# Joining neighbouring short rows into one stored tile, in a pairwise outer-product kernel with batch normalisation

## The chip, the cores and the metric

The kernel runs on one core of a Trainium2 chip. The metric is the device time of one execution in microseconds (us), the median over several runs. Beside it there is one profiled execution, which gives the busy time of the engines (TensorE, VectorE, ScalarE, GpSimd and SyncE, written PE, DVE, ACT, POOL and SP in the profile) and of the transfers.

## The reference

Inputs are `xi` and `xj`, each (1024, 39, 16) in float32: 1024 samples, 39 fields, 16 values. For every pair of fields (r, c) with c < r, 741 pairs in all, the outer product of `xj[:, r]` and `xi[:, c]` is formed, a 16 x 16 block. Each pair is normalised over the samples and the block, scaled by `gamma`, shifted by `beta` and multiplied by one 16 x 16 matrix `W`.

```
rows, cols = tril_indices(39, k=-1)                    # 741 pairs
cross  = xj[:, rows, :, None] * xi[:, cols, None, :]    # (1024, 741, 16, 16)
mean   = mean(cross, axis=(0, 2, 3))
var    = mean((cross - mean)**2, axis=(0, 2, 3))
normed = (cross - mean) * rsqrt(var + 1e-5) * gamma + beta
out    = normed[:, None] * W                            # (1024, 1, 741, 16, 16)
```

The output is 1024 x 741 x 256 x 4 bytes = 777 MB. The inputs are 5 MB.

## The kernel before

**Tiling.** The 1024 samples lie on 128 partitions with 8 samples each. The pairs are taken by row: row r has r pairs, (r, 0) to (r, r-1), and they stand next to each other in the output. A tile is one row for T = 2 of the 8 samples of every partition, so that it holds 2r blocks of 1 KB per partition. A row takes four tiles, for the samples `t0` = 0, 2, 4 and 6.

**The buffer.** All tiles live in one tensor, `y_sb`, of 2 x 76 blocks per partition. Its two halves (`slot`) are used in turn. In each half lie a long row r and the short row 38-r behind it, 38 pairs per sample together, so that a half is always full. The list `tiles` says for each tile its row, its first sample and its place. The order is first the middle row 19, then 20 with 18, then 38 alone, then 37 with 1, 36 with 2, down to 21 with 17. Within a pair of rows it goes long, short, long, short, with `t0` growing. A place is used again by the tile four steps later.

**The work of a tile.** `scale_xi` (GpSimd) multiplies `xi` by the pair's scale into a small tile `xs`, of which there are two. `products` forms the blocks: for each sample and each i of 16 one instruction multiplies `xs` by a scalar of `xj`. ScalarE and GpSimd divide the 16 between them (`split`). Rows 5 to 7 are formed whole on GpSimd, rows 1 to 4 on VectorE. `finish` adds the shift and multiplies by `W`. VectorE does most pairs, each with one `scalar_tensor_tensor` for both samples. A share (`POOL_SHARE`, 0.13 of the row, rounded) is done on GpSimd. `store` then issues the DMAs on SyncE. A tile of a row up to 19 leaves in one DMA for both samples, a longer one in one DMA for each sample. Rows over 30 leave in two pieces, with the last sample stored whole where the row is 36 or less.

**The order.** Nothing is reordered: each engine runs its instructions as they were written. One loop over the tiles writes them, and each step of it forms the products of the tile ahead while the present one is finished:

```
for n in range(1, len(tiles)):
    if n + 2 < len(tiles):
        scale_xi(n + 2)
    finish(n)
    ...          # apply(group), where its tile has come
    if n + 1 < len(tiles):
        products(n + 1)
```

Waits come from overlaps of the regions read and written: the products of a tile wait for the stores that read its place last, and a store waits for the engines that finished its tile.

**Statistics.** Ahead of the loop the means and variances of all pairs come from sums over samples and small matrix products. `spread` copies the coefficients to all partitions by groups of rows (`ROW_GROUPS`), and `apply`, three or four small VectorE instructions, turns a group's coefficients into scale and shift. In the kernel before, each group names the tile at which it is applied.

Line numbers in the profile are those of the kernel before: L148 and L150 are the products on ScalarE and GpSimd, L170 is `scale_xi`, L231 is the store, L294 and L297 are GpSimd's share of `finish`, and L308 is VectorE's.

Of the kernel before, what the change touches and what calls it, by code (L numbers as in the profile page):

```python
# [7 lines left out]
F32 = mybir.dt.float32  # L8
AF = mybir.ActivationFunctionType
ALU = mybir.AluOpType  # L10
# [4 lines left out]
T = 2  # L15
# [12 lines left out]
SHORT, OWN = 4, 1  # L28
# [3 lines left out]


ROW_GROUPS = (
    (19, 20, 0, None), (20, 21, 1, None), (18, 19, 1, 2), (38, 39, 1, 8), (34, 38, 1, 9), (1, 5, 1, 10), (29, 34, 2, 36),
    (5, 10, 2, 37), (25, 29, 3, 76), (10, 14, 3, 77), (21, 25, 4, 108), (14, 18, 4, 109),
)
SHORT_GROUP = 5

# [2 lines left out]
def tile_pair_outer_batchnorm(  # L42
# [24 lines left out]

    half = T * (F - 1)
    mid = (F - 1) // 2
    tiles = [(mid, t0, t0 // T * half // 2) for t0 in range(0, NT, T)]  # L70
    slot = 0
    for r in (mid + 1, *range(F - 1, mid + 1, -1)):
        for t0 in range(0, NT, T):
            tiles.append((r, t0, slot * half))
            if r < F - 1:
                tiles.append((F - 1 - r, t0, slot * half + T * r))
            slot ^= 1

    RAW = 1

# [1 line left out]
    scaled_short = ctx.enter_context(tc.tile_pool(name="scaled_short", bufs=1))  # L82
    scaled = ctx.enter_context(tc.tile_pool(name="scaled", bufs=2))
    psp = ctx.enter_context(tc.tile_pool(name="ps", bufs=1, space=bass.MemoryType.PSUM))
    xi_sb = cpool.tile([P, NT, F, E], F32, name="xi_sb")
    xj_sb = cpool.tile([P, NT, F, E], F32, name="xj_sb")
    w_sb = cpool.tile([P, 1, EE], F32, name="w_sb")
    st_sb = cpool.tile([P, 2, NP], F32, name="st_sb")
    s_sb = st_sb[:, 0:1].unsqueeze(3)
    t_sb = st_sb[:, 1]  # L90
    y_sb = cpool.tile([P, 2 * half, EE], F32, name="y_sb")
    w_dve = psp.tile([P, 1, EE], F32, name="w_dve")

    xi_v = xi.rearrange("(p t) f e -> p t f e", t=NT)
    xj_v = xj.rearrange("(p t) f e -> p t f e", t=NT)
    out_v = out.rearrange("(p t) o n i j -> p t (o n i j)", t=NT)


# [37 lines left out]
    stt = nc.vector.scalar_tensor_tensor  # L136

    def view(n):
        r, _, u = tiles[n]
        return y_sb[:, u : u + T * r, :].rearrange("p (t n) e -> p t n e", t=T)  # L140

    def product(n, engine, t, i, src):

        r, t0, _ = tiles[n]
        y = view(n).rearrange("p t n (i j) -> p t n i j", j=E)[:, t, :, i, :]
        scale = xj_sb[:, t0 + t, r, i : i + 1]
        if engine is nc.scalar:
            nc.scalar.activation(y, src, AF.Copy, scale=scale)  # L148
        else:
            engine.tensor_scalar(y, src, scale, 1.0, ALU.mult, ALU.mult)  # L150

    def raw_products(n, engine, steps):
        r, t0, _ = tiles[n]
        for step in steps:
            t, i = divmod(step, E)
            yield lambda t=t, i=i: product(n, engine, t, i, xi_sb[:, t0 + t, 0:r, :])

    def emit(work, count):
        for _, step in zip(range(count), work):
# [2 lines left out]
    xs_of = {}  # L162

    def scale_xi(n):
        r, t0, _ = tiles[n]
        if r <= SHORT:
            return
        n0 = first[r]
        xs = scaled.tile([P, T, r, E], F32, tag="xs", name=f"xs_{r}_{t0}")
        nc.gpsimd.tensor_tensor(  # L170
            xs,
            xi_sb[:, t0 : t0 + T, 0:r, :],
            s_sb[:, :, n0 : n0 + r, :].to_broadcast([P, T, r, E]),
            ALU.mult,
        )
        xs_of[n] = xs

    def products(n):

        r, t0, _ = tiles[n]  # L180
        if r <= SHORT:
            xs = scaled_short.tile([P, T, r, E], F32, tag="xs_short", name=f"xs_{r}_{t0}")
            nc.vector.tensor_tensor(  # L183
                xs,
                xi_sb[:, t0 : t0 + T, 0:r, :],
                s_short[:, first[r] : first[r] + r]
                .unsqueeze(1)
                .unsqueeze(3)
                .to_broadcast([P, T, r, E]),
                ALU.mult,  # L190
            )
            for t in range(T):
                nc.vector.tensor_tensor(  # L193
                    view(n)[:, t].rearrange("p n (i j) -> p n i j", j=E),
                    xs[:, t].unsqueeze(2).to_broadcast([P, r, E, E]),
                    xj_short[:, t0 + t, r - 1 : r, :].unsqueeze(3).to_broadcast([P, r, E, E]),
                    ALU.mult,
                )
            return
        xs = xs_of.pop(n)  # L200
        if r <= OUTER:
            for t in range(T):
                nc.gpsimd.tensor_tensor(  # L203
                    view(n)[:, t].rearrange("p n (i j) -> p n i j", j=E),
                    xs[:, t].unsqueeze(2).to_broadcast([P, r, E, E]),
                    xj_sb[:, t0 + t, r : r + 1, :].unsqueeze(3).to_broadcast([P, r, E, E]),
                    ALU.mult,
                )
            return
        if n < 3:  # L210
            split = E - POOL_I_FIRST[n]
        elif r > LONG:
            split = E - POOL_I_LONG
        else:
            split = E - (POOL_I_BESIDE if SHORT < F - 1 - r <= OUTER else POOL_I)
        for t in range(T):
            for i in range(E):
                product(n, nc.scalar if i < split else nc.gpsimd, t, i, xs[:, t])

    def store(n, c0, c1, t_from=0, t_to=T):  # L220
        r, t0, _ = tiles[n]
        n0 = first[r]

        whole = n >= len(FIRST_PIECES) and r <= WHOLE
        step = 1 if r > mid and (whole or c1 == r) else t_to - t_from
        for t in range(t_from, t_to, step):
            if whole and step == 1 and t == t_to - 1:
                if c1 < r:
                    continue
                c0 = 0  # L230
            nc.sync.dma_start(  # L231
                out_v[:, t0 + t : t0 + t + step, (n0 + c0) * EE : (n0 + c1) * EE],
                view(n)[:, t : t + step, c0:c1, :].rearrange("p t n e -> p t (n e)"),
            )

    def affine(n, pairs, engines=(nc.scalar, nc.gpsimd)):

        r = tiles[n][0]
        y = view(n)
        for c in pairs:  # L240
            s_c = st_sb[:, 0, first[r] + c : first[r] + c + 1]
            t_c = t_sb[:, first[r] + c : first[r] + c + 1]
            engine = engines[c % len(engines)]
            if engine is nc.scalar:
                nc.scalar.activation(y[:, :, c, :], y[:, :, c, :], AF.Identity, bias=t_c, scale=s_c)  # L245
            else:
                engine.tensor_scalar(y[:, :, c, :], y[:, :, c, :], s_c, t_c, ALU.mult, ALU.add)  # L247
# [14 lines left out]
    def bounds(n):  # L262
        if n < len(FIRST_PIECES):
            return FIRST_PIECES[n]
        r = tiles[n][0]
        if r <= ONE:
            return 0, r

        return 0, r // 2 + max(0, (WHOLE + 1 - r) * 3 // 2), r

    def finish(n):


        r = tiles[n][0]
        n0 = first[r]
        y = view(n)
        long = r > LONG
        p1 = r // 2 if long else r
        if long:
            share = POOL_PAIRS_LONG  # L280
        elif RAW < n < 10:
            share = POOL_PAIRS_FIRST
        else:
            share = int(r * POOL_SHARE + 0.5) if r > SHORT else 0
        p0 = p1 - share
        step = POOL_PAIRS_LONG // 2 if long else r
        for c0 in range(p0, p1, step):
# [30 lines left out]
    with tc.manual_schedule():  # L318
# [2 lines left out]
        def load(engine, to, source, t):  # L321
            engine.dma_start(to[:, t], source[:, t])

        nc.sync.dma_start(xi_sb[:, 0, 0 : F // 2], xi_v[:, 0, 0 : F // 2])
        nc.scalar.dma_start(xi_sb[:, 0, F // 2 : F], xi_v[:, 0, F // 2 : F])
        load(nc.sync, xj_sb, xj_v, 0)
        load(nc.scalar, xi_sb, xi_v, 1)
        load(nc.sync, xj_sb, xj_v, 1)
# [19 lines left out]

        sources = (xj_sb[:, :, 1:F], xi_sb[:, :, 0:G])
        scales = (0.25, 0.25 / NB**0.5)

        def field(x, k):
# [123 lines left out]
        used = [0] * len(ps_st)  # L478

        def spread(group):  # L480
            r0, r1, bank, _ = ROW_GROUPS[group]
            n0, n1 = first[r0], first[r1 - 1] + r1 - 1
            at = used[bank]
            used[bank] = at + 2 * (n1 - n0)
            ps = ps_st[bank][:, at : used[bank]].rearrange("p (x n) -> p x n", x=2)
            for r in range(r0, r1):
                nc.tensor.matmul(  # L487
                    ps[:, :, first[r] - n0 : first[r] - n0 + r],
                    pick[:, r - 1, :],
                    stq[:, :, 0:r],  # L490
                    start=True,
                    stop=True,
                )
            spread_of.append((ps, n0, n1))
# [23 lines left out]
        products(1)  # L518
        scale_xi(2)

        for n in range(1, len(tiles)):
            if n + 2 < len(tiles):
                scale_xi(n + 2)
            finish(n)
            for group, (_, _, _, tile_of) in enumerate(ROW_GROUPS):
                if n == tile_of:
                    apply(group)
            if n + 1 < len(tiles):
                products(n + 1)
            if n == 12:  # L530
                nc.scalar.copy(xj_short, xj_sb[:, :, 1 : SHORT + 1, :])


# [26 lines left out]
```

## Time and profile before

| | |
|---|---|
| median of 3 runs | 1863.88 us (1863.8 to 1863.93) |
| the profiled execution's own time | 1864.56 us |
| its span, first to last instruction | 1862.7 us |
| VectorE busy | 1714.3 us, 92% |
| ScalarE busy | 1576.3 us, 85% |
| GpSimd busy | 1542.9 us, 83% |
| TensorE busy | 34.3 us, 2% |
| written to HBM | 776.99 MB, 420 GB/s over the span |
| packets | 55286 in all, 54928 on SyncE's queue |
| chain that ended last | DMA 53%, ACT 22%, DVE 18%, issue 3% |

Busy time is the time in which an engine has an instruction in it; the mean duration that the profile gives for one instruction is longer than its share of the busy time, since neighbours overlap. A packet is what one DMA engine moves as one piece. The time to landing of a DMA runs from its issue to the signal that it has ended, so that it holds the wait behind earlier transfers. The chain is followed back from the last instruction, at each step to what released it.

### The profile page before, as it was taken

Reading aid. Unit: us, or ns where it says so; the run is one execution under the profiler, and the core shown is the slowest. Engines: PE = TensorE matmul, PEld = TensorE weight load, DVE = VectorE, ACT = ScalarE, POOL = GpSimd, SP = SyncE. Lnnn points to the kernel's source line nnn. Section 1 sums busy time; section 2 is a strip of 40 time slices with the busy share of each in tenths; the row PEclk is TensorE's granted clock in tenths of the full one; section 3 lists DMA queues with packets and bytes.
Section 4 is the critical chain, followed back from the end, with each engine's and each line's share of the span. In section 5 each row is a group of like instructions: output and inputs, shape, how many; then the busy total and the mean of one; then the engine's idle time right before and its main releaser. Section 6 shows DMA issues by size and latency. Waiting matters only on the chain.

```text
span 1862.7 us, 9385 instructions
## 1 busy us (share of the span) xinstructions
PE 34.3 (2%) x212; PEld 33.7 (2%) x212; DVE 1714.3 (92%) x2638; ACT 1576.3 (85%) x3130; POOL 1542.9 (83%) x1655
## 2 busy tenths in 40 slices
PE   7000000000000000000000000000000000000000
PEld 7000000000000000000000000000000000000000
DVE  8999889899999999999999999999999999999994
ACT  8999888888888776666898989999999998989891
POOL 9999777787777789999988888888888888888882
PEclk7555555555555555555555555555555555555555
DMA  7999999999999999999999999999999999999998
GB/s 289 396 421 421 430 427 427 429 424 427 424 428 423 424 424 426 427 425 425 420 428 429 428 430 427 426 427 427 427 431 427 426 428 431 428 425 428 428 428 359
DMA packets 55286, 783.60 MB, mean 421 GB/s; under 512 B 4784, under 2 KB 6448, under 8 KB 18096
## 3 DMA queue, kind: packets, MB, share of 16 engines
q1 hardware_dynamic: 54928, 782.53, 99.2%
q14 instruction: 69, 0.57, 0.1%
q10 hardware_dynamic: 288, 0.48, 0.1%
q8 instruction: 1, 0.02, 0.0%
HBM read 6.00 MB, written 776.99 MB: 420 GB/s over the span
## 4 chain that ended last, share of the span: by engine, by line
DMA 53%; ACT 22%; DVE 18%; issue 3%; POOL 1%; PE 0%; SPq 0%; ACTq 0%; DVEq 0%; POOLq 0%
DMA out_dram<-y_sb 53%; ACT y_sb L148 22%; DVE y_sb L308 17%; POOL y_sb L150 1%; DVE y_sb L364 0%; POOL xs L170 0%; POOL y_sb L247 0%; PE ps L401 0%; SPq L231 0%; DVE y_sb L254 0%; ACTq L148 0%; PE ps L379 0%; DVE y_sb L385 0%; DVE y_sb L371 0%; DVE xs L183 0%
## 5 line engine op out<-in xcount | busy, mean ns | idle before, releaser
L308 DVE SCALAR_TENSOR_TENSOR y_sb<-y_sb,st_sb,w_dve 128x512 f32<-128x512 f32 (+1 forms) x2511 | 1653.1, 740 | 113.3 <-issue 95.9
L148 ACT ACTIVATE y_sb<-xs,xj_sb 128x144 f32<-128x144 f32 (+23 forms) x2930 | 1453.0, 586 | 238.2 <-DMA out_dram<-y_sb 181.6
L297 POOL TENSOR_TENSOR y_sb<-y_sb,w_sb 128x2048 f32<-128x2048 f32 (+3 forms) x155 | 517.4, 3343 | 89.1 <-ACT y_sb L292 79.5
L150 POOL TENSOR_SCALAR y_sb<-xs,xj_sb 128x320 f32<-128x320 f32 (+19 forms) x1006 | 557.4, 577 | 9.8 <-DMA out_dram<-y_sb 9.7
L170 POOL TENSOR_TENSOR xs<-xi_sb,st_sb 128x640 f32<-128x640 f32 (+33 forms) x135 | 183.9, 1362 | 178.8 <-ACT y_sb L148 174.5
L294 POOL TENSOR_SCALAR y_sb<-y_sb,st_sb 128x512 f32<-128x512 f32 x291 | 196.8, 692 | 5.1 <-ACT y_sb L148 5.1
L292 ACT ACTIVATE y_sb<-y_sb,st_sb 128x512 f32<-128x512 f32 x160 | 100.2, 708 | 3.8 <-POOL y_sb L150 2.1
L203 POOL TENSOR_TENSOR y_sb<-xs,xj_sb 128x1280 f32<-128x1280 f32 (+2 forms) x24 | 66.7, 2802 | 0.0
L193 DVE TENSOR_TENSOR y_sb<-xs,ps 128x256 f32<-128x256 f32 (+3 forms) x32 | 24.8, 818 | 0.5
L487 PE MATMUL ps<-y_sb 38*128 38x38 f32 (+37 forms) x76 | 16.4, 397 | 2.4 <-DVE y_sb L473 2.4
L487 PEld LDWEIGHTS ps<-y_sb 38*128 38x128 f32 x76 | 16.3, 329 | 2.5 <-POOL y_sb L150 2.5
L150 POOL TENSOR_SCALAR y_sb<-xi_sb,xj_sb 128x304 f32<-128x304 f32 x24 | 11.9, 514 | 0.0
L254 DVE TENSOR_TENSOR y_sb<-y_sb,w_dve 128x2048 f32<-128x2048 f32 (+4 forms) x6 | 10.8, 1840 | 0.5 <-POOL y_sb L247 0.5
L364 DVE TENSOR_REDUCE y_sb<-y_sb 128x38 f32<-128x608 f32 x14 | 10.4, 781 | 0.0
L247 POOL TENSOR_SCALAR y_sb<-y_sb,st_sb 128x512 f32<-128x512 f32 x9 | 7.0, 786 | 2.2 <-ACT y_sb L148 2.2
L245 ACT ACTIVATE y_sb<-y_sb,st_sb 128x512 f32<-128x512 f32 x9 | 6.5, 803 | 0.3 <-ACT y_sb L148 0.3
L361 ACT ACTIVATE y_sb<-xi_sb 128x608 f32<-128x608 f32 x8 | 5.7, 707 | 1.1 <-DMA xi_sb<-in_r_xi_dram 0.7
L361 ACT ACTIVATE y_sb<-xj_sb 128x608 f32<-128x608 f32 x8 | 5.7, 708 | 1.1 <-DMA xj_sb<-in_r_xj_dram 0.6
L379 PE MATMUL ps<-xi_sb,y_sb 128*128 128x152 f32 x40 | 6.1, 302 | 0.0
L379 PEld LDWEIGHTS ps<-xi_sb,y_sb 128*128 128x128 f32 x40 | 5.8, 202 | 0.0
L401 PE MATMUL ps<-y_sb 128*128 128x128 f32 x24 | 5.5, 428 | 1.0 <-POOL y_sb L319 1.0
L401 PEld LDWEIGHTS ps<-y_sb 128*128 128x128 f32 x24 | 5.2, 331 | 1.0 <-POOL y_sb L319 1.0
(43 smaller groups left out, 50.5 us busy)
## 6 DMA issues: line engine op xcount, KB each, us to landing
out_dram<-y_sb SPq DMA_DIRECT2D x16, 3072.0 KB, 21.9
out_dram<-y_sb SPq DMA_DIRECT2D x20, 2432.0 KB, 12.5
out_dram<-y_sb SPq DMA_DIRECT2D x10, 4608.0 KB, 15.2
out_dram<-y_sb SPq DMA_DIRECT2D x12, 3840.0 KB, 20.8
out_dram<-y_sb SPq DMA_DIRECT2D x16, 2816.0 KB, 22.1
out_dram<-y_sb SPq DMA_DIRECT2D x12, 3584.0 KB, 22.9
out_dram<-y_sb SPq DMA_DIRECT2D x12, 3328.0 KB, 24.3
out_dram<-y_sb SPq DMA_DIRECT2D x15, 2560.0 KB, 12.3
```

The source lines that it names most:

```text
L148: nc.scalar.activation(y, src, AF.Copy, scale=scale)
L150: engine.tensor_scalar(y, src, scale, 1.0, ALU.mult, ALU.mult)
L170: nc.gpsimd.tensor_tensor(xs, xi_sb[:, t0 : t0 + T, 0:r, :], s_sb[:, :, n0 : n0 + r, :].to_broadcast([P, T, r, E]), ALU.mult,)
L193: nc.vector.tensor_tensor(view(n)[:, t].rearrange("p n (i j) -> p n i j", j=E), xs[:, t].unsqueeze(2).to_broadcast([P, r, E, E]), xj_short ...
L203: nc.gpsimd.tensor_tensor(view(n)[:, t].rearrange("p n (i j) -> p n i j", j=E), xs[:, t].unsqueeze(2).to_broadcast([P, r, E, E]), xj_sb[:, ...
L292: nc.scalar.activation(y[:, :, c, :], y[:, :, c, :], AF.Identity, bias=t_c)
L294: nc.gpsimd.tensor_scalar(y[:, :, c, :], y[:, :, c, :], t_c, 1.0, ALU.add, ALU.mult)
L297: nc.gpsimd.tensor_tensor(y[:, :, c0:c1, :], y[:, :, c0:c1, :], w_sb.unsqueeze(1).to_broadcast([P, T, c1 - c0, EE]), ALU.mult,)
L308: stt(y[:, t : t + size, c, :], y[:, t : t + size, c, :], t_sb[:, n0 + c : n0 + c + 1], w_dve.to_broadcast([P, size, EE]), ALU.add, ALU.mult,)
L361: nc.scalar.activation(squares[x][:, t], sources[x][:, t], AF.Square, scale=scales[x])
L379: nc.tensor.matmul(ps, unit, sources[x][:, t0:t1, :, e : e + q], start=e == 0, stop=e + q == E)
L487: nc.tensor.matmul(ps[:, :, first[r] - n0 : first[r] - n0 + r], pick[:, r - 1, :], stq[:, :, 0:r], start=True, stop=True,)
```

## The change

The rows are taken in another order, and some short rows are joined. After 20 with 18 and 38 alone, as before, two long rows r and r-1 (37 and 36, 35 and 34, down to 23 and 22) are taken together with their short rows 38-r and 39-r, which are neighbours and stand next to each other in the output. For each `t0` there are three tiles: row r, row r-1, and one tile with both short rows. The last row, 21 with 17, goes long, long, short, short. There are 120 tiles instead of 152.

The buffer grows by one block, to 153. The long row r lies at block 0, the long row r-1 at block 77. The joined tile lies in the two gaps: its first sample behind row r, its second sample 75 blocks further, behind row r-1. Each sample of it is one run of 77-2r pairs in the buffer and in the output. A place is used again by the tile three steps later (four in the last row).

For a joined tile `scale_xi` and `products` run once for each of its rows, as they did for separate tiles, and `finish` and `store` once for the whole; GpSimd's share is counted from the sum of pairs. Coefficient groups are applied a fixed number of tiles ahead of their first use. The loads leave out the last field of `xi` and the first of `xj`, which are used by no pair.

```diff
-    for r in (mid + 1, *range(F - 1, mid + 1, -1)):
+    for r in (mid + 1, F - 1):
         for t0 in range(0, NT, T):
-            tiles.append((r, t0, slot * half))
+            tiles.append(((r,), t0, slot * half))
             if r < F - 1:
-                tiles.append((F - 1 - r, t0, slot * half + T * r))
+                tiles.append(((F - 1 - r,), t0, slot * half + T * r))
             slot ^= 1
+    for r in range(F - 2, mid + 2, -2):
+        for t0 in range(0, NT, T):
+            tiles.append(((r,), t0, 0))
+            tiles.append(((r - 1,), t0, half + 1))
+            tiles.append(((F - 1 - r, F - r), t0, T * r))
+    r = mid + 2
+    for t0 in range(0, NT, 2 * T):
+        tiles.append(((r,), t0, 0))
+        tiles.append(((r,), t0 + T, half + 1))
+        tiles.append(((F - 1 - r,), t0, T * r))
+        tiles.append(((F - 1 - r,), t0 + T, half + 1 + T * r))
...
-    xi_sb = cpool.tile([P, NT, F, E], F32, name="xi_sb")
-    xj_sb = cpool.tile([P, NT, F, E], F32, name="xj_sb")
+    xi_sb = cpool.tile([P, NT, F - 1, E], F32, name="xi_sb")
+    xj_sb = cpool.tile([P, NT, F - 1, E], F32, name="xj_sb")
...
-    y_sb = cpool.tile([P, 2 * half, EE], F32, name="y_sb")
+    y_sb = cpool.tile([P, 2 * half + 1, EE], F32, name="y_sb")
...
     def view(n):
-        r, _, u = tiles[n]
-        return y_sb[:, u : u + T * r, :].rearrange("p (t n) e -> p t n e", t=T)
+        rows, _, u = tiles[n]
+        if len(rows) > 1:
+            apart = y_sb[:, 2 : 2 * half, :].rearrange("p (t n) e -> p t n e", t=T)
+            return apart[:, :, u - 2 :]
+        return y_sb[:, u : u + T * sum(rows), :].rearrange("p (t n) e -> p t n e", t=T)
+
+    def parts(n):
+        at = 0
+        for r in tiles[n][0]:
+            yield r, at, at + r
+            at += r
...
     def scale_xi(n):
...
+        xs = scaled.tile([P, T, sum(rows), E], F32, tag="xs", name=f"xs_{rows[0]}_{t0}")
+        for r, c0, c1 in parts(n):
+            n0 = first[r]
+            nc.gpsimd.tensor_tensor(
+                xs[:, :, c0:c1, :],
                 xi_sb[:, t0 : t0 + T, 0:r, :],
+                s_sb[:, :, n0 : n0 + r, :].to_broadcast([P, T, r, E]),
                 ALU.mult,
             )
...
     def products(n):
+        for r, c0, c1 in parts(n):
...
             for t in range(T):
+                for i in range(E):
+                    engine = nc.scalar if i < split else nc.gpsimd
+                    product(n, r, c0, engine, t, i, xs[:, t, c0:c1])

     def store(n, c0, c1, t_from=0, t_to=T):
-        r, t0, _ = tiles[n]
-        n0 = first[r]
+        rows, t0, _ = tiles[n]
+        n0, r = first[rows[0]], sum(rows)
...
     def bounds(n):
...
-        if r <= ONE:
+        rows = tiles[n][0]
+        r = sum(rows)
+        if r <= ONE or len(rows) > 1:
             return 0, r
...
     def finish(n):
-        r = tiles[n][0]
-        n0 = first[r]
+        rows = tiles[n][0]
+        n0, r = first[rows[0]], sum(rows)
...
-            share = int(r * POOL_SHARE + 0.5) if r > SHORT else 0
+            share = int(r * POOL_SHARE + 0.5) if rows[-1] > SHORT else 0
...
+        due = {}
+        for group, (r0, r1, _) in enumerate(ROW_GROUPS[2:], 2):
+            use = min(n for n, tile in enumerate(tiles) if any(r0 <= r < r1 for r in tile[0]))
+            due.setdefault(use - 3 if group == 2 else use - 4, []).append(group)
+
...
-            for group, (_, _, _, tile_of) in enumerate(ROW_GROUPS):
-                if n == tile_of:
-                    apply(group)
+            for group in due.get(n, ()):
+                apply(group)
```

## The prediction

> **What bounds the kernel now.** I read first the page's slices (forty equal parts of the span; digits are busy tenths):
>
> ```profile
> DVE  8999889899999999999999999999999999999994
> ACT  8999888888888776666898989999999998989891
> POOL 9999777787777789999988888888888888888882
> DMA  7999999999999999999999999999999999999998
> GB/s 289 396 421 421 430 427 427 429 424 427 424 428 423 424 424 426 427 425 425 420 428 429 428 430 427 426 427 427 427 431 427 426 428 431 428 425 428 428 428 359
> DMA packets 55286, 783.60 MB, mean 421 GB/s; under 512 B 4784, under 2 KB 6448, under 8 KB 18096
> ```
>
> From the third slice to the last but one the transfers stand at 420 to 431 GB/s while ScalarE moves between 6 and 9 tenths: the rate doesn't follow the engines. The 777 MB of output set the time; only the first two slices and the drain fall short. VectorE, 92% of the span, is second. Next the longest waits, and SyncE's own:
>
> ```profile
> ACT y_sb L148 <- DMA out_dram<-y_sb: 181.6, 82, 6.7
> POOL xs L170 <- ACT y_sb L148: 174.5, 67, 6.3
> SPq L231 <- DVE y_sb L308: 1428.0, 175, 18.4
> ```
>
> ScalarE's products wait for stores to leave the buffer, and SyncE waits for VectorE, not for room in its queue. Whether there is slack is shown by the timeline of the last stage (start, length, engine, operation) and its stores' time to landing:
>
> ```profile
> 1768.50 21.18 ACT L148 ACTIVATE y_sb<-xs,xj_sb 128x272 f32<-128x272 f32 x48 [2.24 <-DVE y_sb L308]
> 1778.59 9.97 DVE L308 SCALAR_TENSOR_TENSOR y_sb<-y_sb,st_sb,w_dve 128x512 f32<-128x512 f32 x15 [0.31 <-issue]
> 1789.77 11.94 DVE L308 SCALAR_TENSOR_TENSOR y_sb<-y_sb,st_sb,w_dve 128x512 f32<-128x512 f32 x18 [1.21 <-issue]
> 1791.93 21.18 ACT L148 ACTIVATE y_sb<-xs,xj_sb 128x272 f32<-128x272 f32 x48 [2.24 <-DVE y_sb L308]
> ```
>
> ```profile
> out_dram<-y_sb SPq DMA_DIRECT2D x2, 4352.0 KB, 26.5
> ```
>
> Starts recur every 23.43 us, the drain of one 38-row pair of tiles. A 17-row tile needs 10.4 us at 428 GB/s but lands 26.5 us after issue: some 16 us of finished work lie ahead of it. That backlog is what a late tile may eat before the time changes.
>
> Last, does the number of packets matter to a saturated queue? The transfers in four windows: 365 to 640 and 640 to 905 us (rows 36 to 31, stored in more pieces), 940 to 1385 and 1385 to 1830 us (rows 30 to 21):
>
> ```profile
> DMA packets 8172, 117.07 MB, mean 426 GB/s; under 512 B 750, under 2 KB 750, under 8 KB 3650
> DMA packets 8049, 112.96 MB, mean 426 GB/s; under 512 B 722, under 2 KB 722, under 8 KB 4094
> DMA packets 10794, 190.17 MB, mean 427 GB/s; under 512 B 927, under 2 KB 927, under 8 KB 927
> DMA packets 10761, 190.42 MB, mean 428 GB/s; under 512 B 913, under 2 KB 913, under 8 KB 913
> ```
>
> The first two together: 540 us, 230.03 MB, 16221 packets, so 2.348 us and 70.5 packets per MB. The last two: 890 us, 380.59 MB, 21555 packets, so 2.338 us and 56.6 packets per MB. Slope: 0.0090 us / 13.9 packets = **0.65 ns of queue time per packet**; without packets 2.3015 us per MB, or 434.5 GB/s.
>
> **What the Trainium skill says.** "DMA: Bandwidth & Descriptors", Specifications, gives a fabric ceiling of 435 GB/s; my intercept of 434.5 agrees. The same page under Bandwidth gives about 10.5 ns per packet, measured on loads issued by GpSimd; 0.65 ns with 16 engines side by side is 10.4 ns on each, and its section on small descriptors explains a fixed cost per packet. Anatomy of one DMA there puts about 2.0 us of fixed cost, mostly completion, on each transfer of that path; here the quickest store lands 2.2 us after issue.
>
> **The change part by part.**
>
> *Packets.* Each run of pairs of one sample is one packet, and each DMA adds 16 small ones. The counts prove it: the stores' 47872 runs + 20 loads x 128 + 299 DMAs x 16 = 55216, what queues q1 and q10 show (54928 + 288). Joining rows 1 with 2 up to 15 with 16 takes away 8 x 1024 = 8192 runs. Stores fall from 279 to 259 (64 short tiles with one store each become 32; the 12 of 23, 27 and 31 pairs are longer than 19 and go out sample by sample, so 44 stores): 20 x 16 = 320 packets. Gain 8512 x 0.65 = **5.5 us**. Low bound: nothing, if the windows differ for another reason; high bound: the window 265 to 340 us (2612 packets, 31.74 MB) (row 37) against the last two gives 24.5 ns / 25.7 packets = 0.95 ns, or 8.1 us. I take 0.65, from the longest windows.
>
> *Loads.* 16 loads shrink by 8 KB: 0.13 MB, 0.3 us at 421 GB/s, ahead of a start that waits mostly on reductions. I take 0.2.
>
> *Engines.* Joined rows 5+6 give GpSimd one pair (11 x 0.13, rounded) where two tiles gave one each: 4 more L308 on VectorE, at 1639.8/2477 = 0.66 us, together 2.6 us, and 4 L294 and 24 L297 fewer on GpSimd (the other shares are equal in sum, multiplied in one instruction instead of two). In 50 us windows VectorE is 93 to 95% busy there; the backlog covers it, and without that cover it costs 2.6. Coefficient groups are applied 3 to 4 tiles ahead of their use, two of them (rows 34 to 37, 1 to 4) later than before, some 3 us of the same instructions on VectorE, covered likewise. The 20 issues saved (0.38 us each) lie in SyncE's waiting. The products are the same in number and size.
>
> *The joined tile's turnaround.* This is where a wait can appear. The order becomes long, long, short instead of long, short, long, short. A tile now reuses the place of the tile three back, not four; the bytes between are the same 152 pairs, 46.4 us of draining. But a tile's own drain, products and finishing must fit into that, and the joined one is up to 31 pairs. The tightest stage is 23, 22 and 15+16, four rounds. Take the moment when the old joined tile has landed as 0. The queue holds 45 pairs of the long tiles, 45 x 0.61 = 27.5 us; less 2 us for issue and completion, the new stores must be issued by **25.4**.
> - ScalarE: row 15's first sample is done before 0. Its second: 12 x 0.391 (busy 37.5 us / 96 of that form) = 4.7. Row 16: 24 x 0.403 (38.7/96) = 9.7, done at 14.5. In the built program VectorE's first instruction on row 15 waits for row 15's products alone.
> - GpSimd then: L170 1.4, four adds 2.7 (0.676 each), L297 on 4 pairs 4.5, done at 23.1; then eight products of the next 23-row tile, 4.4, done at 27.6. Behind these queue the next scaling and, on VectorE, that tile.
> - VectorE: the two long tiles, 20 + 19 instructions, 25.8 us from 27.6: to 53.4. Less one round of 46.4, it starts the joined tile at 7.0; its 27 instructions, 17.9 us, end at **24.9**.
> So 0.5 us are left, where the kernel before had 16. Stage 25, 24, 13+14 has about 4 us (finished near 24, due at 28), stage 27 about 11. I price this at 0, with bounds 0 and 4 x 2 = 8 us: 2 us is the sum of what gaps between instructions (0.3 to 1.2 in the timeline) could add to that round. It can't bring a gain.
>
> Sum: 1864.56 (the profiled execution; 1.86 around its span of 1862.7) - 5.5 - 0.2 = 1858.9; it stood 0.7 above the median of 1863.88, so **1858.2**.
>
> **Rivals.**
> 1. *Packets are free* (12%). Against: two independent pairs of windows give the slope, and the ceiling fits. For: the four rates differ by 0.4% only, and stages differ in more than packets. Then 1863.7.
> 2. *The joined tile comes late: slower* (18% that it costs over 2 us, 12% that the end is over 0.2% slower). Each round of the last paired stage leaves the queue empty. If VectorE could start row 15 only when row 16's products are done, it would end at 14.5 + 17.9 = 32.4, 7 us late: 4 rounds x 7 = 28, and 0.3 x 4 in the stage before, so 1863.9 - 5.7 + 29 = 1887. The built waits speak against that; a lateness of part of it doesn't need it. It decides from 5.7/4 = 1.4 us per round (gain gone) or (5.7 + 3.7)/4 = 2.4 us (slower).
> 3. *VectorE becomes the bound* in rows 37 to 32 (8%), where 50 us windows from 350 to 750 us show it 90 to 99% busy. Then the gain of these 12 of 32 rounds, 2.1 us, stays unused, and the 4 added instructions come on top: 1858.2 + 2.1 + 2.6 = 1862.9. Against: the rate keeps 422 to 433 GB/s in just these windows.
>
> The remaining 62% is the forecast.
>
> **How the numbers follow.** 0.2%, 3.7 us, is about what a measurement of this kernel can tell from no change. Faster by more than that: the forecast and the small cases of lateness, 0.68. Within: rivals 1 and 3 and a lateness of about 1 us, 0.20. Slower: 0.12. Range 1854.5 (8.1 us of packets, 0.3 of loads, 1 for the drain's own spread) to 1864 (packets free, or lateness of 1.4 us); about 1 in 10 lies above.
>
> **What would show it.** Packets 46774 and under 8 KB 12656; 429 to 430 GB/s from 200 to 1800 us; time to landing of the joined tiles falling from stage to stage to about that of their own 19 us plus 2; L308 x4 more. Wrong if a slice near 1500 to 1760 us falls under 420 GB/s with the chain on L308 or L148 (rival 2), or if the rate stays at 426 to 428 with the fewer packets (rival 1).

## The result and the profile after

The changed kernel takes **2025.5 us** (median of 4 runs, 2025.36 to 2025.96) where the kernel before took 1863.91 beside it: a ratio of 1.087, 95% interval 1.085 to 1.089. The profiled execution took 2025.56 us, with a span of 2023.8. The forecast was 1858.2, its range 1854.5 to 1864. L168, L170, L191, L255, L319, L322 and L333 of the changed kernel are L148, L150, L170, L231, L294, L297 and L308 of the kernel before.

The page of the changed kernel, in forty slices of 50.6 us, with the packets below:

```profile
DVE  8999788999999687676678676669999899899994
ACT  8998888888877544675555876669998999899892
DMA  7999999999999977777977777987999999999999
GB/s 300 399 423 423 425 414 429 428 427 427 427 434 421 416 305 322 317 307 326 394 324 303 315 313 321 385 358 314 430 428 433 425 432 432 417 424 424 425 430 390
DMA packets 46775, 783.47 MB, mean 387 GB/s; under 512 B 4464, under 2 KB 5104, under 8 KB 12656
```

The packets are those forecast, to within one. The loss is not spread out. Slices 14 to 27 (counted from 0; 708 to 1417 us) run at 303 to 394 GB/s, and all others about as before. In all of those slices but the last VectorE and ScalarE fall to between 4 and 8 tenths, so no engine has become the bound. Those slices are the rows 33 to 28 and the step to 26, whose joined tiles have 11, 15 and 19 pairs. The place that the prediction watched, 1500 to 1760 us, shows nothing of the kind (417 GB/s at the least).

Its longest waits (engine, line, what was waited for: total us, times, longest us):

```profile
ACT y_sb L168 <- DMA out_dram<-y_sb: 344.6, 58, 26.4
POOL xs L191 <- ACT y_sb L168: 225.0, 39, 12.2
DVE y_sb L333 <- issue: 213.3, 31, 16.1
```

There are fewer waits of ScalarE for a store than before (58 against 82), but they hold 344.6 us instead of 181.6, and the longest has grown from 6.7 to 26.4. The waits of GpSimd for ScalarE, and of VectorE, stand behind that one. The timeline of ScalarE in rows 33 and 32 (start, length, instructions; in brackets the idle time before and what ended it):

```profile
709.60 16.38 ACT L168 ACTIVATE y_sb<-xs,xj_sb 128x528 f32<-128x528 f32 x26 [2.17 <-POOL xs L191]
750.87 16.02 ACT L168 ACTIVATE y_sb<-xs,xj_sb 128x512 f32<-128x512 f32 x26 [24.89 <-DMA out_dram<-y_sb]
769.06 16.38 ACT L168 ACTIVATE y_sb<-xs,xj_sb 128x528 f32<-128x528 f32 x26 [2.17 <-POOL xs L191]
810.93 16.02 ACT L168 ACTIVATE y_sb<-xs,xj_sb 128x512 f32<-128x512 f32 x26 [25.49 <-DMA out_dram<-y_sb]
```

The products of row 33 (128x528) start at once. Those of row 32 (128x512) wait 25 us for a store, every round, and the round takes 60 us instead of 46.4. The transfers of 700 to 800 us, in slices of 2.5 us, show what that wait does:

```profile
DMA  9999000007998999969999899999000008999999
GB/s 509 433 433 433 0 0 0 0 0 301 452 396 351 583 433 419 419 288 433 433 397 424 356 415 572 433 433 433 0 0 0 0 0 358 396 452 405 476 419 419
```

The queue is not slow, it is empty: 12.5 us of zeros in every round, and about 430 GB/s between them. The products of row 32 wait for the joined tile's store, and while they wait only row 33's tile is left to be drained.

**What they wait for.** Row 32's new tile goes to block 77, where nothing but row 32's old tile lay. In the built program its products wait for more: for the store of the joined tile of the round before. The trace agrees: this store has landed at 750.64 and 810.82 us, and the products start at 750.87 and 810.93. That store is one DMA for both samples, two runs of 11 pairs at block 66 and, 75 blocks further, at block 141. Block 77 lies between the runs and belongs to neither. The waits are derived from overlaps, and here the store is treated as if it read everything from its first byte to its last. So row 32 gets a wait that no shared byte asks for. Joined tiles of 15 and 19 pairs give the same wait. Those of 23, 27 and 31 pairs leave in one DMA for each sample, a single run without a gap, and give none. Those of 3 and 7 pairs, though stored in two runs, have no such wait in the built program either. Why is open, so this is not shown to hold for every DMA of two distant runs. Twelve tiles wait in this way: row 32 three times, rows 30 and 28 four times each, row 26 once.

**What that costs.** The wait closes a loop: VectorE's finishing of row 32 up to its first stored piece (15.2 us), the drain of its tile and of the joined one with the completion behind it (26.3 + 2), the next products of row 32 (16.0) make 59.5 us, against 46.4 of draining. That is 13.1 us for each round; worked out the same way, 14.7 for row 30, 13.9 for row 28 and 13.3 for row 26. Together 3 x 13.1 + 4 x 14.7 + 4 x 13.9 + 13.3 = 167 us, less the 5.7 of the forecast's gain 161. Measured: 161.6. That the two agree so closely is luck: the gain that was subtracted did not come (first experiment below). There the waits are worth 2025.5 - 1865.1 = 160.4 us, so the price of 167 was 4% high.

### The profile page after: what moved, and what is told of

The parts are those of the page before. It is cut to its first block, busy times and chain, and to the rows that moved or that the text cites. A ratio compares the mean times of both kernels' runs of the same rounds, so it can differ in the third digit from the quotient of the medians.

```text
span 2023.8 us, 9235 instructions
## 1 busy us (share of the span) xinstructions
PE 33.1 (2%) x212; PEld 32.3 (2%) x212; DVE 1714.4 (85%) x2642; ACT 1571.5 (78%) x3130; POOL 1530.2 (76%) x1627
## 2 busy tenths in 40 slices
DMA packets 46775, 783.47 MB, mean 387 GB/s; under 512 B 4464, under 2 KB 5104, under 8 KB 12656
## 5 line engine op out<-in xcount | busy, mean ns | idle before, releaser
L333 DVE SCALAR_TENSOR_TENSOR y_sb<-y_sb,st_sb,w_dve 128x512 f32<-128x512 f32 (+1 forms) x2515 | 1653.2, 739 | 274.7 <-issue 213.3
L168 ACT ACTIVATE y_sb<-xs,xj_sb 128x576 f32<-128x576 f32 (+23 forms) x2930 | 1448.3, 587 | 405.0 <-DMA out_dram<-y_sb 344.6
L170 POOL TENSOR_SCALAR y_sb<-xs,xj_sb 128x320 f32<-128x320 f32 (+21 forms) x1006 | 557.0, 578 | 116.2 <-DMA out_dram<-y_sb 80.5
L322 POOL TENSOR_TENSOR y_sb<-y_sb,w_sb 128x2048 f32<-128x2048 f32 (+2 forms) x131 | 508.3, 3887 | 86.1 <-ACT y_sb L317 78.5
L191 POOL TENSOR_TENSOR xs<-xi_sb,st_sb 128x640 f32<-128x640 f32 (+33 forms) x135 | 182.9, 1363 | 248.1 <-ACT y_sb L168 225.0
L319 POOL TENSOR_SCALAR y_sb<-y_sb,st_sb 128x512 f32<-128x512 f32 x287 | 193.5, 692 | 7.2 <-ACT y_sb L168 7.2
L512 PEld LDWEIGHTS ps<-y_sb 38*128 38x128 f32 x76 | 15.2, 309 | 2.5 <-POOL y_sb L170 2.5
L170 POOL TENSOR_SCALAR y_sb<-xi_sb,xj_sb 128x304 f32<-128x304 f32 x24 | 11.9, 514 | 0.0
L389 DVE TENSOR_REDUCE y_sb<-y_sb 128x38 f32<-128x608 f32 x14 | 10.4, 780 | 0.0
```

Source lines behind the costliest of these rows:

```text
L191: nc.gpsimd.tensor_tensor(xs[:, :, c0:c1, :], xi_sb[:, t0 : t0 + T, 0:r, :], s_sb[:, :, n0 : n0 + r, :].to_broadcast([P, T, r, E]), ALU.mult,)
L319: nc.gpsimd.tensor_scalar(y[:, :, c, :], y[:, :, c, :], t_c, 1.0, ALU.add, ALU.mult)
L322: nc.gpsimd.tensor_tensor(y[:, :, c0:c1, :], y[:, :, c0:c1, :], w_sb.unsqueeze(1).to_broadcast([P, T, c1 - c0, EE]), ALU.mult,)
L333: stt(y[:, t : t + size, c, :], y[:, t : t + size, c, :], t_sb[:, n0 + c : n0 + c + 1], w_dve.to_broadcast([P, size, EE]), ALU.add, ALU.mult,)
L512: nc.tensor.matmul(ps[:, :, first[r] - n0 : first[r] - n0 + r], pick[:, r - 1, :], stq[:, :, 0:r], start=True, stop=True,)
```

## Experiments

Ratios are to the kernel before, run beside each kernel, whose median was 1864.1 to 1864.4 us. The letter W in the expectations stands for the theory just told. Its rivals put the loss on the new order, with three steps instead of four until a place is used again (T), or on the two-run DMA itself (D).

### Both samples of a joined tile in two DMAs

```diff
-        step = 1 if r > mid and (whole or c1 == r) else t_to - t_from
+        step = 1 if len(rows) > 1 or r > mid and (whole or c1 == r) else t_to - t_from
```

> Every joined tile is stored sample by sample, so no store reads two stretches that lie apart; nothing else is changed (20 DMAs more). Theory W (a store of two samples that lie apart is taken to read everything between them, so that the next round's tile of row r-1 waits for it; 12 rounds of 13 to 15 us, 167 us in all): 2025.5 - 167 = 1858.5, transfers at 429 to 430 GB/s throughout. Theory T (the order long, long, short with a place reused three tiles later leaves too little time in rows 33 to 27): stays above 2000. Theory D (one DMA with samples 75 KB apart moves more slowly): about 1858 too, but then the rate in the slow rounds, not idle time, must have been low.

Measured: 1865.06 us (13 runs), ratio 1.0005 (0.9997 to 1.0014). One condition in the store takes away 160 us: order, places, products and runs are those of the changed kernel. Its page:

```profile
GB/s 293 396 423 422 425 429 414 425 427 434 427 429 427 416 414 428 428 425 425 429 428 432 428 433 430 430 429 428 428 429 415 424 424 430 421 413 428 424 427 386
DMA packets 47095, 783.47 MB, mean 421 GB/s; under 512 B 4784, under 2 KB 5424, under 8 KB 12976
```

The hole at 700 to 1400 us has gone. But the forecast gain hasn't come: 8191 packets fewer than the kernel before, and the time is the same. That is the second question, below.

### The same for the 11-pair tiles alone

```diff
+        step = 1 if rows == (5, 6) or r > mid and (whole or c1 == r) else t_to - t_from
```

> Only the joined rows 5+6 (11 pairs, four tiles) are stored sample by sample; 8 of the 12 rounds keep the wait. Theory W: the four rounds return 3 x 13.1 + 14.7 = 54 us: 1971. Theory T: 2025.

Measured: 1972.0 us (one run), 53.5 less than the changed kernel. The cost of the wait is local to the stage of this joined tile, and comes out as priced (54).

### The reverse: all joined tiles in one DMA for both samples

```diff
+        step = 1 if len(rows) == 1 and r > mid and (whole or c1 == r) else t_to - t_from
```

> All joined tiles, those of 23, 27 and 31 pairs too, are stored with both samples in one DMA, so that 24 rounds have the wait and one tile of row 21. Theory W: a round there is finishing of row r-1 (15.2, 13.9, 12.6 us), the drain of it and of the joined tile (30.0, 31.2, 32.5), 2 us, and the products (12.5, 12.3, 11.6): 59.7, 59.4 and 58.7 instead of 46.4 to 46.8; 4 x (13.3 + 13.0 + 12.0) = 153 us more: 2178. Theory T: 2025, since the order is the same. Theory D: more than 2025, without idle transfers.

Measured: 2192.23 us (one run), 14 above the number. The stages that were free of the wait get it as soon as their tiles leave in one DMA. The excess of 14 us lies almost wholly in one stage: after their waits ScalarE's products of rows 26 and 24 start 59.5 to 60.6 us apart, about as priced, those of row 22 and the step to 21 62.6 to 63.5 instead of 58.7. This is the stage whose turnaround the prediction found tightest; what adds the 4 us was not tested.

### The joined tile's samples next to each other

The places are changed instead of the store: row r at block 0, the joined tile behind it with both samples together, row r-1 at the end of the buffer. The store is one DMA again, but now without a gap.

```diff
-            tiles.append(((r - 1,), t0, half + 1))
+            tiles.append(((r - 1,), t0, 2 * half - T * (r - 1)))
...
-        if len(rows) > 1:
-            apart = y_sb[:, 2 : 2 * half, :].rearrange("p (t n) e -> p t n e", t=T)
-            return apart[:, :, u - 2 :]
```

> The joined tile's two samples lie next to each other between the two long rows (row r at block 0, joined tile behind it, row r-1 at the end); the stores, their number and their form in the output are those of the changed kernel, two samples in one DMA up to 19 pairs. Theory W: no tile lies between the samples, so 1858.3. Theory T (order and reuse distance): above 2000, since both are kept. Theory D (two samples in one DMA): near 2025 if the distance in the buffer doesn't matter, 1858 if it does.

Measured: 1891.98 us (4 runs), ratio 1.015. The order is the changed kernel's and the joined store is one DMA, yet 134 us of the loss are gone. So neither the order nor one DMA for both samples is to blame, but the gap. W's number, 1858.3, was missed by 34 us all the same: the kernel stays 28 us above the kernel before. The trace points to another wait. At each step from one pair of long rows to the next, row r-1 moves up by 4 blocks and truly overlaps the part of the old tile that is stored last. The transfers of 440 to 520 us, over the first of these steps that show it, in slices of 2 us, and ScalarE's wait there (L165 is this kernel's line of the products):

```profile
GB/s 418 580 313 557 313 571 218 507 370 451 417 415 589 312 556 305 556 305 22 0 172 344 516 344 426 426 557 279 544 331 505 322 430 500 338 481 174 369 492 410
```

```profile
454.93 14.16 ACT L165 ACTIVATE y_sb<-xs,xj_sb 128x544 f32<-128x544 f32 x22 [8.86 <-DMA out_dram<-y_sb]
```

The queue runs empty in this way four times, near 478, 672, 867 and 1058 us, and the windows of 186 us around these places (466 to 1210 us) lose 7 to 10 us each. No run tests this reading. The changed kernel's gap avoids such an overlap: there every row r-1 lies at block 77.

### Where do 5.7 us go: fewer joins, other shares, more packets

Five kernels, all with the joined tile stored sample by sample, ask why the gain fails to come.

Joining only down to long row 26, with rows 25 to 21 going long, long, short, short:

```diff
-    for r in range(F - 2, mid + 2, -2):
+    for r in range(F - 2, mid + 6, -2):
...
+    for r in range(mid + 6, mid + 1, -1):
```

> As the version stored sample by sample, but only short rows 1 to 12 are joined (long rows 37 to 26); rows 25 to 21 go long, long, short, short as row 21 does. Theory R (the rounds with 27 and 31 joined pairs turn round too late: 2.9 and 3.2 us over the drain's own pace in these two stages): these 6 us come back, 2048 more runs cost 1.3 us: 1865.1 - 6.1 + 1.3 = 1860.3. Rival P (the rate there is low for another reason, the packets' form or the state of the queue): about 1865 to 1866.

Measured: 1865.46 us (13 runs), ratio 1.0005 (0.9997 to 1.0014). Theory R's number was missed by 5 us.

More of the joined tiles for VectorE and less for GpSimd in two stages, and the other way in the late long rows:

```diff
+            if r in (27, 31) and len(rows) > 1:
+                share -= 2
+            elif rows[0] in (25, 24, 23, 22):
+                share += 1
```

> As the version stored sample by sample, but in the rounds with 27 and 31 joined pairs GpSimd finishes 2 pairs of the joined tile instead of 4, and 1 more of each of the two long tiles; VectorE's sum is the same. Theory R: what is late is GpSimd's queue behind the joined tile (scaling, its pairs, then the next tile's products, on which VectorE waits 3.3 to 4.2 us); 3.5 us of it are taken away, so most of the 6 us in the two stages come back: 1860 (1859 to 1862). Rival P: 1865.

Measured: 1865.05 us (13 runs), ratio 1.0003 (0.9995 to 1.0012). Theory R's number was missed by 5 us here as well; shifting single pairs between the engines in these stages changes nothing.

The joined tile stored row by row and sample by sample, 9216 runs and small packets more:

```diff
+        if len(rows) > 1:
+            for _, a0, a1 in parts(n):
+                for t in range(t_from, t_to):
+                    nc.sync.dma_start(...)
+            return
```

> As the version stored sample by sample, but every joined tile is stored row by row: 8192 runs and 64 DMAs more, 9216 packets, everything else the same. Theory K (a packet costs 0.65 ns of a full queue): 6.0 us more, 1871.1. Rival F (packets are free): 1865. Where the queue isn't full (two stages of eight) a part may be hidden: 1869.5 at least.

Measured: 1868.74 us (11 runs), ratio 1.0024 (1.0015 to 1.0033).

Rows 30 to 22 stored in two pieces for each sample, 10368 packets more:

```diff
+            cut = (c0, (c0 + c1) // 2, c1) if len(rows) == 1 and mid + 2 < r <= ONE else (c0, c1)
+            for a0, a1 in zip(cut, cut[1:]):
```

> As the version stored sample by sample, but each sample of the long rows 30 to 22 is stored in two DMAs of half a row, issued together: 9216 runs and 72 DMAs more, 10368 packets. Theory K: 6.7 us more, 1871.8, at least 1869.5 with a part hidden in the last two paired stages. Rival F: 1865.

Measured: 1869.25 us (9 runs), ratio 1.0025 (1.0016 to 1.0035). Packets are not free, then, but the totals are below the forecast's 6.0 and 6.7 us: each against the kernel before beside it, these two lie 3.4 and 3.9 us above the sample-by-sample kernel, 0.37 and 0.38 ns for each added packet. (Such a total also holds what else moved with the packets; see the table below.)

What a packet costs can also be read where no stage disturbs: 1024 to 1397 us, 373 us in rows 29 to 26. The transfers there, of the kernel before, of the sample-by-sample kernel and of the one with halved long rows:

```profile
DMA packets 9010, 159.65 MB, mean 428 GB/s; under 512 B 780, under 2 KB 780, under 8 KB 780
```

```profile
DMA packets 6983, 160.11 MB, mean 429 GB/s; under 512 B 782, under 2 KB 782, under 8 KB 782
```

```profile
DMA packets 11528, 159.02 MB, mean 426 GB/s; under 512 B 1278, under 2 KB 1278, under 8 KB 1278
```

373 us over the MB give 2.3364, 2.3296 and 2.3456 us per MB at 56.4, 43.6 and 72.5 packets per MB: 0.53 and 0.55 ns per packet from the middle one (0.35 from the row-by-row kernel, 9254 packets and 159.77 MB). The queue does get faster with fewer packets, here by 0.3%. So the gain exists in this stage and is given back elsewhere.

### Joining rows 7 to 12 alone

Long rows 37 to 32 and 25 to 21 go back to the order of the kernel before.

```diff
+    for r in range(F - 2, mid + 1, -1):
+        if mid + 6 < r < mid + 13:
+            ...          # three tiles for each pair of long rows, as in the change
+        for t0 in range(0, NT, T):
+            u = t0 // T % 2 * (half + 1)
+            tiles.append(((r,), t0, u))
+            tiles.append(((F - 1 - r,), t0, u + T * r))
```

> Short rows 7 to 12 alone are joined (long rows 31 to 26), stored sample by sample; long rows 37 to 32 and 25 to 21 keep the order of the kernel before. 3 x 1024 = 3072 runs fewer, same number of stores, 0.13 MB of loads fewer: about 52214 packets. Theory A (the gain of the sample-by-sample version was eaten where its rate fell, about 3.5 us in rows 37 to 32 and 6 us in rows 25 to 22, both stages now back in the old order): the gain left is 3072 x 0.40 to 0.65 ns = 1.2 to 2.0 us and 0.2 of loads, so 1861.9 to 1862.7, 1.4 to 2.2 below the kernel before. Theory S (the slowest of the 16 transfer engines sets the end, and what the average engine saves goes into a thinner tail): 1863.9 to 1864.5, no difference, with the rate of each stage back at that of the kernel before or better, and the spread between a store's first and last engine at the end above the 6.9 us of the kernel before.

Measured: 1874.37 us (5 runs), ratio 1.0055 (1.0041 to 1.0068), above both numbers. The stages themselves came out as theory A said: no loss in rows 37 to 32, none in 25 to 22. What neither theory had are the two steps between the orders: 3.5 us near 840 to 1020 us and 11 us at the second. The places don't fit there, and at the second step ScalarE waits 14.8 us for a store (until 1389.77 us); no run tests whether that is the cause. The transfers of that second step, 1385 to 1425 us in slices of 1 us, also show something else:

```profile
DMA  8999999999999999999993999999991000000000
GB/s 377 400 471 565 424 400 401 406 408 408 433 410 435 410 410 410 563 461 512 461 410 156 411 412 425 425 413 426 426 386 67 27 27 27 13 16 0 0 0 0
```

The queue runs dry, but not at once: it falls from 386 to 67, and 13 to 27 GB/s go on for five slices. By an estimate from the full rate, 430 / 16, one engine moves 27 GB/s. So most of the 16 transfer engines are done, and one still works off its share.

### Work for TensorE that nobody reads

This follows from the last picture: transfer engines that are late hold back a store's completion. Fetching instructions (queues q8 and q14 of the page) could be what makes single engines late.

```diff
+        for _ in range(3000):
+            nc.tensor.matmul(ps_s[0:8, 0:1], w_sb[:, 0, 0:8], w_sb[:, 0, 0:1], start=True, stop=True)
```

> The kernel before with 3000 tiny matrix products (8x1, into a PSUM bank that nothing reads) added on TensorE after its last use: no engine, store or buffer of the output work is touched. What it adds is instructions to fetch: 6000, by the 0.57 MB for 9385 instructions of the kernel before 0.37 MB or some 45 packets of 8 KB in the instruction queue. Theory I (the late engines are late because the instruction fetches are theirs: 0.57 MB at 27.2 GB/s of one engine are 21 us, and in the kernel before the 16 engines end together 19.6 us late, counted from the first, 18 of it on four of them): the sum rises by about 13 us to 33, and the end comes between 3 us later (spread over the same four) and 7 to 13 us later (on one), 1867 to 1877. Theory N (the lateness has nothing to do with fetches): sum near 20, time 1864.1.

Measured: 1887.08 us (4 runs), ratio 1.0123 (1.0106 to 1.014): 23 us for work on an engine that is otherwise idle. Its page:

```profile
PE   8545545000000000000000000000000000000000
GB/s 295 394 421 372 380 393 403 395 427 423 430 424 429 424 428 424 425 426 426 425 420 428 428 428 428 430 429 426 430 426 428 429 427 426 430 427 430 427 429 355
q8 instruction: 48, 0.79, 0.2%
q14 instruction: 69, 0.57, 0.1%
```

TensorE runs in slices 0 to 6. The rate falls to 372 to 403 GB/s in slices 3 to 7, where the kernel before has 421 to 430, and queue q8 carries 47 more packets, 0.77 MB, the last at 330 us. (12000 instructions were added, not 6000, so twice the bytes that the expectation counted.) With 0.1% of the bytes, they cost 1.2% of the time. From 150 to 340 us the trace shows one engine's signal 5 to 12 us behind the first of its store. After the last fetch the engines are together again (1.1 us at 470 to 650 us), and at the end the sum of their lateness is 20.2 us, which is theory N's number; the time is that of neither theory. So fetches do make single engines late and cost time under a full queue, but the lateness of early fetches isn't carried to the end. That it is the fetching and not the products themselves is argued from the late engine and from q8; no run has one without the other.

## Why the prediction was wrong

**The step that failed** is in "The joined tile's turnaround": "A tile now reuses the place of the tile three back, not four; the bytes between are the same 152 pairs". It took each wait to be given by the place alone. For the tiles of 11, 15 and 19 pairs the products of row r-1 wait for the joined tile as well, because its one DMA spans block 77. I had looked up the built waits only in the last stages, where the joined tiles are longer than 19 pairs and leave sample by sample. In those stages there is no such wait, and in the others I assumed what I had seen there. Both halves of the cause stood in my own description: samples 75 blocks apart, and one DMA for both up to 19 pairs.

**Rival 2** (12%) had the sign and the waiting line, L148 behind a store, but another mechanism, place and price: it expected VectorE to be late with rows 15 and 16 and 28 us near the end. The loss was 161.6 us between 708 and 1417 us.

**Without the false wait** the forecast would have been 1858.2 and the time 1865.06. This miss can be split. For each kernel I take, in eight windows of 186 us from 280 to 1769 us, the time over the prediction's own model (2.3015 us per MB + 0.65 ns per packet), and at the end the tail: how much later than the mean of the 16 engines the last one signals for the last stores (5.75 us in the kernel before). All in us against the kernel before; loads are -0.3 in each:

| kernel | packets x 0.65 ns | lost in the windows | tail | sum with loads | measured |
|---|---|---|---|---|---|
| sample by sample | -5.3 | +9.1 | -2.7 | +0.8 | +1.0 |
| joined to row 12 | -4.0 | +3.2 | +2.0 | +0.9 | +1.1 |
| other shares | -5.3 | +9.3 | -3.2 | +0.5 | +0.7 |
| row by row | +0.7 | +1.4 | +2.2 | +4.0 | +4.4 |
| long rows halved | +1.4 | +5.3 | -2.6 | +3.8 | +4.9 |
| rows 7 to 12 alone | -2.0 | +15.2 | -3.1 | +9.8 | +10.3 |

This is bookkeeping, and would nearly close with another price for a packet too. It says where the time lies, not why. Term by term:

- *Packets, -5.5.* The count was right (46775 against 46774). The price was high: 0.35 to 0.55 ns instead of 0.65, so 3 to 4.7 us. Rival 1, packets free, falls. The prediction took support from the Trainium skill ("DMA: Bandwidth & Descriptors", Bandwidth), whose about 10.5 ns per packet it set beside its own 10.4. But the page's figure comes from a whole DMA, 0.67 us for 64 packets, and the 10.4 ns are the time on each of 16 engines: the two are not the same quantity, and that they nearly agree supports nothing.
- *Turnaround, priced 0 with a bound of 8.* In the sample-by-sample kernel the windows of rows 25/24 and 23/22 (1397 to 1769 us) lose 6.1 us, against 0.0 before. VectorE's timeline there:

```profile
1560.40 43.54 DVE L333 SCALAR_TENSOR_TENSOR y_sb<-y_sb,st_sb,w_dve 128x512 f32<-128x512 f32 x66 [2.68 <-POOL y_sb L170]
1608.17 43.54 DVE L333 SCALAR_TENSOR_TENSOR y_sb<-y_sb,st_sb,w_dve 128x512 f32<-128x512 f32 x66 [4.23 <-POOL y_sb L170]
1654.98 43.54 DVE L333 SCALAR_TENSOR_TENSOR y_sb<-y_sb,st_sb,w_dve 128x512 f32<-128x512 f32 x66 [3.27 <-POOL y_sb L170]
```

  All 66 instructions of a round run in one piece after a wait for GpSimd's products of the next long tile, the chain that the prediction wrote down. From start to start it is 47.8 and 46.8 us, where the drain takes 46.4: late by 1.4 and 0.4 us a round, with 0.5 counted on. But that this chain sets the pace is not shown. With the other shares VectorE waits for GpSimd's products 1.1 us at most in rows 23/22, yet its rounds start 47.8, 46.8 and 46.8 us apart (from 1559.68 us on), and these windows lose the same 6.1 us. Nor is the spacing new: two steps of 23.43 us in the kernel before make 46.9. The bound of 8 held the loss; the 0 that I took did not. Where the joined tile leaves row by row, or isn't joined in these stages, the loss is gone (-0.1 and 0.0 us), so storing it whole brings the loss; by which wait stays open.
- *Rows 37 to 32 (rival 3's place).* The sample-by-sample kernel loses 3.5 us there, and the one with these rows in the old order none. Rival 3 had put 4.7 us on it with VectorE as the bound. That the order brings it is shown; that VectorE is the bound is not, since no run changed its share in these rows.
- *The tail*, which the prediction's sum didn't have (its range holds 1 us for the drain's own spread). It took the mean of the 16 engines for the queue. The end of the program waits for the last of them. The last 33 us (1835 to 1868) of the kernel before, and of the one joined to row 12:

```profile
DMA  9999999999998899889988932121000000000000
GB/s 407 412 433 417 417 417 417 443 443 443 412 590 384 353 458 495 364 343 511 485 359 359 591 127 106 84 127 63 42 21 42 0 0 0 0 10 0 0 0 0
```

```profile
DMA  8999899889997988998899312110000000000000
GB/s 374 495 448 385 364 490 469 385 359 549 401 401 338 591 380 380 464 485 380 359 549 401 148 84 106 84 63 21 21 42 21 21 21 0 0 0 10 0 0 0
```

  The second kernel's full rate ends one slice earlier, its thin tail two slices later. In the kernel before 12 engines end within 0.2 us, and the other four 2.4, 4.0, 4.7 and 6.8 us after the first; in the second, 2.3, 3.4, 4.3 and 8.8. The Trainium skill says in "DMA: Bandwidth & Descriptors" (Why a DMA increments its semaphore by 16 and not by 1) that the engines of one DMA finish independently and that only the full 16 mean that the data has landed; the trace agrees, and gives the size. The kernels whose queue ran short on the way, with 5 us or more lost in the windows, end with 2.6 to 3.2 us of tail instead of 5.8. This fits late engines that catch up while the others wait.

**Right:** that transfers bound the kernel, and the counts of packets and of L333 (2515, four more). The 429 to 430 GB/s did not come, even after 1417 us: the slices there run at 417 to 433, 427 in the mean, the last one left out.

**Open.** What makes the four engines late at the end isn't settled. In the kernel before the sum of their lateness grows by 13 us between 1109 us and the end; 31 instruction fetches of some 0.32 us lie in that time, 9.8 us in all. That would be most of it, but the run with added TensorE work shows only that fetches can do so. What slows rows 37 to 32 in the new order is open too, and so is the wait behind the loss in rows 25 to 22. None of the kernels here is faster than the kernel before.

## What to carry to other kernels

Before counting on a buffer scheme, list for each stage, and not for one of them, which store each write waits for in the built program; a transfer of two distant runs may be ordered as if it covered all between them (here with runs of 11 pairs and more, not with 3 and 7), and one DMA for each run takes that away. Here the stall shows as zeros in the rate with full speed between them, not as a lower rate. And under a full queue count the slowest transfer engine, not the mean: a saving of a few tenths of a per cent can be swallowed by a margin of half a microsecond per round or by the last engine's tail.

## What the runs showed of the hardware

- A store's 16 completion signals spread from 0.8 us (200 to 470 us) to 6.9 us (end) in a run whose queue never empties. They are together again where the queue empties: at 1109 to 1400 us of the changed kernel, with a gap every 60 us, the median spread is 0.2 us, in the kernel before 2.6.
- 47 packets of instructions for an idle engine, 0.77 MB, cost 23 us under a full store queue, some 0.5 us each. The Trainium skill ("Runtime: NRT & Kernel Launch", Instruction fetch mechanics) gives blocks of 16 KiB and calls the cost of crossing into the next block mostly hidden. The size agrees for q8 (0.79 MB / 48 = 16.4 KB), while packets of q14 are half as large (0.57 MB / 69 = 8.3 KB). Under this full queue the cost was not hidden: the stores bore it.
- A further store packet costs 0.35 to 0.55 ns of a full queue (1024 to 1397 us of the kernels above), not 0.65.
